# Scans of an attention and state-space block: diagonals of B through a DRAM buffer, three of eight token tiles

## The chip, the cores and the metric

The kernel runs on one core of a Trainium2 chip. The time is the device time of one execution in microseconds, from the chip's own clock; a lower one is better. All data are 32-bit floats.

## The reference

The input is an image of 256 x 256 tokens with 128 channels. Layer 0 adds row attention with four heads, layer 1 a two-dimensional state-space block; each works on a group-normed input. Nearly all the time goes to the scans of layer 1. The tokens are read in four orders k (by rows, by columns, and both backwards). For each order, each of 256 channels d and each of 16 states n, over the 65536 tokens t:

```python
def step(h, inp):
    d_t, x_t, B_t, C_t = inp
    dA = jnp.exp(d_t[..., None] * As)
    h = dA * h + (d_t * x_t)[..., None] * B_t[:, :, None, :]
    y = jnp.einsum('bkdn,bkn->bkd', h, C_t)
    return (h, y)
```

Here d_t = softplus(dts + dt_b) is a rate for each channel and token, x_t the token's 256 values, B_t and C_t are 16 numbers for each token. The four results are added, normed and projected back.

## The kernel before

The kernel has stages one after the other: statistics and norms, attention, a 3x3 convolution with the projections (`conv`), a transposition of a small array in DRAM (`swap`), the scans (`scans`), the output. The change is in `scans`; between the stages go arrays in DRAM, of which `bk` (B, one row of 16 floats for each token), `xk` (x), `dc0` and `dcT` (the low-rank rates and C) and `y` (the sum of the results) matter here.

**Tiling.** An order k is cut into 64 blocks of TB = 1024 tokens, which are NJ = 8 token tiles of 128. So there are 256 blocks. The first four and the last six blocks of an order are written out, the 54 between are three passes of a hardware loop over 18 blocks. Channels come in NH = 2 halves of 128, on the partitions of the scan. The work of a block is 32 units u = (state m, half h), each with these steps:

- `decay` (L837): ScalarE makes dA = exp(delta * A) for 1024 tokens, 4 units ahead.
- `scale` (L830): ScalarE makes what the turn needs, 3 states ahead. For the first DJ = 4 token tiles it writes into `dg` a diagonal 128 x 128 matrix with B of state m, that is the identity scaled per partition (L833). For the other four it writes into `but` the tile of d_t * x_t scaled by B (L835). In each half it does two of either.
- `turn` (L841): TensorE brings B * d * x to channels x tokens in PSUM, one unit ahead: a matmul of `dxt` with the diagonal for tiles below DJ (L846), a transposition of `but` for the others (L848). A matmul of floats stands as two instructions in the trace, a transposition as one.
- `recur` (L853): VectorE scans 1024 tokens (L858) and keeps the last state (L863); after the second half GpSimd multiplies both halves by C (L865), which `fetch` (L825) has loaded and spread over 128 partitions into one of four `cc` buffers, 3 to 4 states ahead.
- `collect` (L869): TensorE transposes the products and adds them up in PSUM over the states, three states behind (L617).

**The next block's preparation** is laid into the units of the present one (`begin`, L737): the rates by TensorE in units 6, 8, 18 and 20, a softplus from steps on ScalarE in units 6 to 12, on GpSimd in 11 to 14 and on VectorE in 18 and 20, its turn and the product with x in 22 and 24. These rates and turned rates use the same two PSUM buffers (`mms`) as the turns.

**Queues.** The order is written out by hand; every engine takes its instructions in that order. All loads and the store of y are issued by SP's queue, in the order in which the body names them: at unit 0 `load_tokens` for the next block (bt at L727, xk at L728, a megabyte), at unit 8 the store of the block before's y (L902, a megabyte), at 16 the load of y (L948, a megabyte), at 21 the rates (L724), and in each odd unit the cc for four states on (L826). A DMA whose target is not yet free keeps SP, and all that is behind it, waiting. The `dg`, `but` and `cc` rings have four buffers each, `da` and `hs` six.

Of the kernel before, what the change touches and what calls it, by code (L numbers as in the profile page):

```python
# [29 lines left out]
AF = mybir.ActivationFunctionType  # L30
# [5 lines left out]
P = 128  # L36
N = 256
# [4 lines left out]
NH = DI // P  # L42
DS = 16
# [576 lines left out]
def scans(tc, io, c):  # L620
# [11 lines left out]
    nc = tc.nc  # L632
    TB = 1024
    NJ = TB // P
# [5 lines left out]
    with tc.tile_pool(name="e_w", bufs=1) as wp, tc.tile_pool(name="e_1", bufs=1) as sb1, tc.tile_pool(  # L640
# [11 lines left out]
        def ring(name, n, shape, pool=wp):  # L652
            return [pool.tile(shape, F32, name=f"{name}{i}") for i in range(n)]

        DJ = NJ // 2
        xks = ring("xk", 1, [P, NJ, DI])

        dts = ring("dt", 1, [P, TB])
# [5 lines left out]
        ccs = ring("cc", 4, [P, TB])  # L664
        dgs = ring("dg", 4, [P, DJ, P])
        bus = ring("but", 4, [P, NJ - DJ, DI])
        das = ring("da", DA, [P, TB])
        hss = ring("hs", HS, [P, NH, TB])
# [16 lines left out]
        class Block:  # L685
# [39 lines left out]

            def load_tokens(self):
                nc.sync.dma_start(out=self.as_rows(self.bt), in_=self.rows(io["bk"][self.S.k]))  # L727
                nc.sync.dma_start(out=self.as_rows(self.xk), in_=self.rows(io["xk"]))  # L728

            def advance(self, now, after):  # L730
                if self.pieces is None:
                    self.pieces = begin(self)
                while self.pieces and self.pieces[0][:2] <= (now, after):
                    _, _, f, *args = self.pieces.pop(0)
                    f(*args)
# [89 lines left out]
        def fetch(B, m):  # L825
            nc.sync.dma_start(out=ccs[m % 4], in_=B.S.C[m : m + 1, B.where()].partition_broadcast(P))  # L826

        def scale(B, m, h):  # L830
            dg, bu = dgs[m % 4], bus[m % 4]
            for j in range(h * DJ // 2, (h + 1) * DJ // 2):
                nc.scalar.activation(dg[:, j, :], c.ident, AF.Copy, scale=B.bt[:, B.slot(j), m : m + 1])  # L833
                at = B.slot(DJ + j)
                nc.scalar.activation(bu[:, j, :], B.dxt[:, DJ + j, :], AF.Copy, scale=B.bt[:, at, m : m + 1])  # L835

# [4 lines left out]
        def turn(B, m, h):  # L841
            d1 = B.d1 = mm()
            dg, bu = dgs[m % 4], bus[m % 4]
            hc = slice(h * P, (h + 1) * P)
            for j in range(DJ):
                nc.tensor.matmul(d1[:, j * P : (j + 1) * P], B.dxt[:, j, hc], dg[:, j, :], start=True, stop=True)  # L846
# [6 lines left out]
        def recur(B, m, h):  # L853
            hs = hss[(B.n * DS + m) % HS]
            o, d0, d1 = hs[:, h, :], das[((B.n * DS + m) * NH + h) % DA], d1s.pop(0)
            if B.S.back:
                o, d0, d1 = o[:, ::-1], d0[:, ::-1], d1[:, ::-1]
            nc.vector.tensor_tensor_scan(o, d0, d1, state[:, m, h : h + 1], ALU.mult, ALU.add)  # L858
            if h == NH - 1:

                last = 0 if B.S.back else TB - 1
                last = hs[:, :, last : last + 1]
                nc.vector.tensor_reduce(state[:, m, :], last, AX.X, ALU.max)  # L863
                for x in range(NH):
                    nc.gpsimd.tensor_tensor(hs[:, x, :], hs[:, x, :], ccs[m % 4], ALU.mult)  # L865
# [16 lines left out]
        def collect_some(most):  # L882

            for x in list(waiting):
                if most == 0:
                    break
                B, _, _, j = x
                if B.slot(j) // PB in B.free:
                    waiting.remove(x)
                    collect(*x)  # L890
                    most -= 1

        def evict(B, after, part):

            n = NJ // PB // 2
            for g in range(part * n, (part + 1) * n):
                to = B.y[:, g * PB : (g + 1) * PB, :]
                nc.vector.tensor_tensor(to, to, pys[g], ALU.add)
                if after:
                    after.free.add(g)  # L900
            if part == 1:
                nc.sync.dma_start(out=B.rows(io["y"]), in_=B.as_rows(B.y))  # L902
# [5 lines left out]
        def body(blocks, before, after):  # L908

            own = len(blocks)  # L910
            at_hand = dict(enumerate(blocks + after))
            if before:
                at_hand[-1] = before
                before.free = before.started = set(range(NJ // PB))
                d1s[:] = [mms[count[0] % 2]]

            def at(u):
                x, s = divmod(u, U)
                return (at_hand[x], *divmod(s, NH)) if x in at_hand else None

            def do(f, u):
                if at(u):
                    f(*at(u))

            if before is None:
                blocks[0].load()
                blocks[0].load_tokens()
                blocks[0].advance(U, True)
                blocks[0].free = set(range(NJ // PB))
                blocks[1].load()  # L930
                for m in range(4):
                    fetch(blocks[0], m)
                for u in range(3 * NH):
                    do(scale, u)
                for u in range(4):
                    do(decay, u)
                do(turn, 0)
            for x, B in enumerate(blocks):
                nxt = at_hand.get(x + 1)
                for s in range(U):  # L940
                    u = x * U + s
                    m, h = divmod(s, NH)
                    if s == 0 and nxt:
                        nxt.load_tokens()
                    if s == 21 and x + 2 in at_hand:
                        at_hand[x + 2].load()
                    if s == 16:
                        nc.sync.dma_start(out=B.as_rows(B.y), in_=B.rows(io["y"]))  # L948
                    if nxt:
                        nxt.advance(s, False)  # L950
                    recur(B, m, h)
                    do(turn, u + 1)
                    if at(u - LAG * NH):
                        waiting.extend((*at(u - LAG * NH), j) for j in range(NJ))
                    collect_some(len(waiting) if s == LAG * NH - 1 else share.get(s, 10))
                    if x - 1 in at_hand and s in (6, 8):
                        evict(at_hand[x - 1], B, (s - 6) // 2)
                    if nxt:
                        nxt.advance(s, True)
                    do(decay, u + 4)  # L960
                    if u == 0:
                        nc.scalar.preload_act_table_set("natural_log_exp_and_others")
                    do(scale, u + 3 * NH)
                    if h == NH - 1 and at(u + 1 + 3 * NH):
                        fetch(*at(u + 1 + 3 * NH)[:2])
            if not after:
                waiting.extend((*at(u), j) for u in range(own * U - LAG * NH, own * U) for j in range(NJ))
                collect_some(len(waiting))
                for part in range(2):
                    evict(blocks[-1], None, part)  # L970
            assert not waiting
# [3 lines left out]
        passes = (n - 2) // LOOP  # L975
        first = (n - passes * LOOP) // 4 * 2
        order = [Scan(x, k) for x, k in enumerate((0, 2, 1, 3))]
        for x, S in enumerate(order):
            starts = [Block(S, b) for b in range(first)]
            ends = [Block(S, b) for b in range(first + passes * LOOP, n)]  # L980
            with tc.manual_schedule():
                nc.vector.memset(state, 0.0)
                body(starts, Block(order[x - 1], n - 1) if x else None, [Block(S, first + i) for i in range(2)])
            with tc.For_i(0, passes, 1, name=f"scan{S.k}") as it, tc.manual_schedule():  # L984
                body(
                    [Block(S, first + i, it) for i in range(LOOP)],
                    Block(S, first - 1, it),
                    [Block(S, first + LOOP + i, it) for i in range(2)],
                )
            with tc.manual_schedule():  # L990
                body(
                    ends,
                    Block(S, first + LOOP - 1, passes - 1),
                    [Block(order[x + 1], i) for i in range(2)] if x + 1 < len(order) else [],
                )


def output(tc, io, c):
# [73 lines left out]
    "dc1": (KD // 2 * RC, NT),  # L1072
    "dcT": (KD // 2 * RC, NT),
    "y": (NT, DI),
}


# [56 lines left out]
```

## Time and profile before

| | |
|---|---|
| median of 3 runs | 28440.62 us (28439.84 to 28441.89) |
| profiled execution | span 28447.5 us; no time beyond it is listed |
| busy: PE, DVE, ACT, POOL | 94%, 88%, 89%, 81% of the span |
| granted TensorE clock | 0.965 |
| DMA | 3630.07 MB, mean 128 GB/s; 1923996 packets |
| scans (L858), count and mean | 8192 of 2340 ns |
| diagonals on ACT (L833) | 16384 of 390 ns, 6393.1 us busy |
| scaled tiles on ACT (L835) | 16384 of 497 ns, 8150.2 us busy |

PE is TensorE, DVE VectorE, ACT ScalarE, POOL GpSimd and SP SyncE; PEld is the loading of TensorE's weights. A line such as L858 is a line of the kernel. In a row of a group the numbers behind the bar are the busy time in us and the mean ns of one instruction, then the time that the engine was idle just before them, and what ended most of it. In a timeline the columns are the start in us from the beginning of the span, the time that the row takes, the engine, the line, the operation, output and inputs, and how many instructions were merged; in square brackets the idle time before it and what ended it. ACT's instructions overlap a little, so that a unit's time is read from start to start. In a row of a DMA queue stand its packets, the MB and the share of sixteen engines' time. The scans take the span from about 4740 us to 27660 us.

### The profile page before, as it was taken

What the parts mean: (1) busy time and instruction counts of PE and PEld (TensorE: products, weight loads), DVE (VectorE), ACT (ScalarE), POOL (GpSimd) and SP (SyncE); (2) the same over time, 40 slices, a digit from 0 to 9 for tenths busy, and PEclk for the clock granted to TensorE, in tenths of its full rate; (3) what the DMA queues carried; (4) which work ended last, traced back from release to release, by engine and by line L of the source; (5) the groups of instructions that cost most, each with busy time, mean ns of one, the idle gap of its engine ahead of it and who ended that gap; (6) DMA issues with size and microseconds to landing.
All of it is one profiled execution on the core that took longest, in us unless ns stands there. A gap on an engine that the chain in (4) does not pass through costs nothing. (4 is left out here: it accounts for less than half of the span.)

```text
span 28447.5 us, 528099 instructions
## 1 busy us (share of the span) xinstructions
PE 26610.1 (94%) x196490; PEld 22529.2 (79%) x196490; DVE 24922.2 (88%) x24253; ACT 25332.4 (89%) x49673; POOL 22944.4 (81%) x10118
## 2 busy tenths in 40 slices
PE   8999996999999999999999999999999999999998
PEld 3555444888888888888888888888888888888884
DVE  4777665999999999999999999999999999999987
ACT  6875224999999999999999999999999999999987
POOL 2443002999999999999999999999999999999983
PEclk9999998999999999999999999999999999999999
DMA  5112345433433333333334333333333333333335
GB/s 206 55 50 71 111 116 115 132 132 129 133 130 133 132 131 132 132 131 132 128 132 133 131 133 132 131 132 129 132 132 130 133 132 129 132 130 132 133 132 172
DMA packets 1923996, 3630.07 MB, mean 128 GB/s; under 512 B 532297, under 2 KB 1240009, under 8 KB 1889490
## 3 DMA queue, kind: packets, MB, share of 16 engines
q1 hardware_dynamic: 1424722, 3339.77, 34.6%
q10 hardware_dynamic: 496640, 255.88, 3.2%
q8 instruction: 1568, 25.69, 0.4%
q14 instruction: 1066, 8.73, 0.1%
HBM read 3002.42 MB, written 592.84 MB: 126 GB/s over the span
## 5 line engine op out<-in xcount | busy, mean ns | idle before, releaser
L865 POOL TENSOR_TENSOR hs<-hs,cc 128x1024 f32<-128x1024 f32 x8192 | 19202.5, 2380 | 1346.1 <-DVE state L863 679.9
L858 DVE TENSOR_TENSOR_SCAN hs<-da,state,mm 128x1024 f32<-128x1024 f32 x8192 | 18976.6, 2340 | 1465.4 <-PE mm L848 1074.7
L846 PE MATMUL mm<-dg,dxt 128*128 128x128 f32 x65536 | 9305.0, 287 | 1065.1 <-DVE hs L858 886.1
L846 PEld LDWEIGHTS mm<-dg,dxt 128*128 128x128 f32 x65536 | 8328.4, 199 | 2257.9 <-DVE hs L858 1897.8
L839 ACT ACTIVATE da<-delta,A 128x1024 f32<-128x1024 f32 x8192 | 9328.4, 1139 | 112.2 <-PEq L984 76.0
L617 PE MATMUL y<-ident,hs 128*128 128x128 f32 x65536 | 8511.4, 275 | 1.4 <-POOL hs L865 1.4
L835 ACT ACTIVATE but<-dxt,bt 128x256 f32<-128x256 f32 x16384 | 8150.2, 497 | 11.4 <-DVE dxt L794 11.4
L617 PEld LDWEIGHTS y<-ident,hs 128*128 128x128 f32 x65536 | 7494.1, 143 | 1.9 <-POOL hs L865 1.9
L833 ACT ACTIVATE dg<-ident,bt 128x128 f32<-128x128 f32 x16384 | 6393.1, 390 | 0.2
L848 PE MATMUL mm<-ident,but 128*128 128x128 f32 x32768 | 5092.5, 280 | 0.0
L848 PEld LDWEIGHTS mm<-ident,but 128*128 128x128 f32 x32768 | 4011.4, 146 | 0.0
L750 PE MATMUL mm<-dt,dtw 9*128 9x512 f32 x4096 | 2033.0, 615 | 265.9 <-DMA bt<-mid_bk 184.5
L385 POOL TENSOR_TENSOR an<-ex,rs 128x1024 f32<-128x1024 f32 x512 | 970.2, 1895 | 1024.5 <-PE tp L394 566.3
L780 POOL TENSOR_TENSOR lw<-lw,e 128x1024 f32<-128x1024 f32 x512 | 1207.7, 2384 | 336.3 <-ACT lw L766 336.3
L750 PEld LDWEIGHTS mm<-dt,dtw 9*128 9x128 f32 x4096 | 680.7, 184 | 959.5 <-issue 733.3
L500 POOL MEMSET pad<- 128x10 f32 x32 | 3.7, 117 | 1650.0 <-PE ps L537 1639.9
L777 POOL TENSOR_TENSOR lw<-lw,w 128x1024 f32<-128x1024 f32 x512 | 1202.9, 2375 | 0.0
L537 PE MATMUL ps<-pad,w 128*128 128x512 f32 x2048 | 954.8, 610 | 161.0 <-ACT xi L525 161.0
L372 ACT ACTIVATE ex<-sc,nm 128x256 f32<-128x256 f32 x2048 | 1013.7, 499 | 0.4
L759 ACT ACTIVATE e<-mm 128x1024 f32<-128x1024 f32 x512 | 524.7, 1025 | 522.1 <-PE mm L750 521.9
L355 DVE CUSTOM_DVE_ANT_0 sc<-ps,bias 128x256 f32<-128x256 f32 x2048 | 746.2, 421 | 117.3 <-PE ps L340 117.3
L394 PEld LDWEIGHTS tp<-ident,an 128*128 128x128 f32 x4096 | 467.5, 141 | 470.7 <-POOL an L385 235.1
(137 smaller groups left out, 18522.4 us busy)
## 6 DMA issues: line engine op xcount, KB each, us to landing
cc<-mid_dc SPq DMA_DIRECT2D x2048, 512.0 KB
cc<-mid_dcT SPq DMA_DIRECT2D x2048, 512.0 KB
xk<-mid_xk SPq DMA_DIRECT2D x256, 1024.0 KB
yb<-mid_y SPq DMA_DIRECT2D x256, 1024.0 KB
mid_y<-yb SPq DMA_DIRECT2D x256, 1024.0 KB
xt<-mid_xT SPq DMA_DIRECT2D x64, 1024.0 KB
mid_xk<-xk ACTq DMA_DIRECT2D x32, 2048.0 KB
mid_y<-y ACTq DMA_DIRECT2D x32, 2048.0 KB
```

The source lines that it names most:

```text
L372: nc.scalar.activation(exs[u][:, x, :], scs[u][:, e, jt, :], AF.Exp, scale=-1.0, bias=nms[u][:, e, jt : jt + 1], accum_out=sms[u][:, x : x ...
L617: nc.tensor.matmul(out, in_, c.ident, is_transpose=True, start=start, stop=stop, skip_group_check=True)
L750: nc.tensor.matmul(pu[:, q : q + T], dtw[0 : DR + 1, k, h * P : (h + 1) * P], B.dt[0 : DR + 1, q : q + T], start=True, stop=True,)
L777: nc.gpsimd.tensor_tensor(B.lw[:, h, :], B.lw[:, h, :], B.w[:, h, :], ALU.add)
L780: nc.gpsimd.tensor_tensor(B.lw[:, h, :], B.lw[:, h, :], B.e[:, h, :], ALU.add)
L833: nc.scalar.activation(dg[:, j, :], c.ident, AF.Copy, scale=B.bt[:, B.slot(j), m : m + 1])
L835: nc.scalar.activation(bu[:, j, :], B.dxt[:, DJ + j, :], AF.Copy, scale=B.bt[:, at, m : m + 1])
L839: nc.scalar.activation(da, B.delta[:, h, :], AF.Exp, scale=A[:, B.S.k * NH + h, m : m + 1])
L846: nc.tensor.matmul(d1[:, j * P : (j + 1) * P], B.dxt[:, j, hc], dg[:, j, :], start=True, stop=True)
L848: nc.tensor.transpose(d1[:, j * P : (j + 1) * P], bu[:, j - DJ, hc], c.ident)
L858: nc.vector.tensor_tensor_scan(o, d0, d1, state[:, m, h : h + 1], ALU.mult, ALU.add)
L865: nc.gpsimd.tensor_tensor(hs[:, x, :], hs[:, x, :], ccs[m % 4], ALU.mult)
```

## The change

Three of the eight token tiles, instead of four, go through a diagonal (DJ = 3), and ScalarE makes none of them; it scales the five others, two in the first half of a state and three in the second. The diagonals come from a new DRAM array `dgd` with two parts, one for even and one for odd blocks; a part holds for each of the 16 states a matrix of 128 rows by 3 x 128 columns. Before the scans SP writes zeros into all of it. In `load_tokens`, between the loads of bt and xk, a new function `spread` issues three DMAs from DRAM to DRAM: each takes the 128 tokens by 16 states of one token tile from `bk` and writes every element into its place on the diagonal, a single float each, 2048 of them. The other places are zero from the start and stay so. `diagonal` then loads a state's whole 128 x 384 matrix into one of the four `dg` buffers (1536 bytes a partition, 192 KB). It is issued by SP in the even units after the scale, three states ahead, and for the first three states of all before the first unit.

```diff
@@ -652,7 +652,7 @@
         def ring(name, n, shape, pool=wp):
             return [pool.tile(shape, F32, name=f"{name}{i}") for i in range(n)]
 
-        DJ = NJ // 2
+        DJ = 3
         xks = ring("xk", 1, [P, NJ, DI])
 
         dts = ring("dt", 1, [P, TB])
@@ -725,7 +725,27 @@
 
             def load_tokens(self):
                 nc.sync.dma_start(out=self.as_rows(self.bt), in_=self.rows(io["bk"][self.S.k]))
+                self.spread()
                 nc.sync.dma_start(out=self.as_rows(self.xk), in_=self.rows(io["xk"]))
+
+            def diagonals(self):
+                return io["dgd"][self.b % 2]
+
+            def spread(self):
+                d = self.diagonals()
+                of = io["bk"][self.S.k]
+                G = N // P
+                with nc.allow_non_contiguous_dma(reason="one element of B per diagonal place"):
+                    for j in range(DJ):
+                        if self.S.across:
+                            x = of.rearrange("(g p w) c -> p g w c", p=P, w=N)
+                            x = x[:, j % G, self.where(N), :][:, j // G, :]
+                        else:
+                            x = of[self.where(), :].rearrange("(j p) c -> p j c", p=P)[:, j, :]
+                        to = bass.AP(
+                            d.tensor, d.offset + j * P, ((DJ * P + 1, P), (P * DJ * P, DS), (1, 1))
+                        )
+                        nc.sync.dma_start(out=to, in_=x.unsqueeze(2))
 
             def advance(self, now, after):
                 if self.pieces is None:
@@ -825,12 +845,15 @@
         def fetch(B, m):
             nc.sync.dma_start(out=ccs[m % 4], in_=B.S.C[m : m + 1, B.where()].partition_broadcast(P))
 
+        def diagonal(B, m):
+            nc.sync.dma_start(out=dgs[m % 4].rearrange("p j q -> p (j q)"), in_=B.diagonals()[m])
+
 
 
         def scale(B, m, h):
-            dg, bu = dgs[m % 4], bus[m % 4]
-            for j in range(h * DJ // 2, (h + 1) * DJ // 2):
-                nc.scalar.activation(dg[:, j, :], c.ident, AF.Copy, scale=B.bt[:, B.slot(j), m : m + 1])
+            bu = bus[m % 4]
+            nb = NJ - DJ
+            for j in range(h * nb // 2, (h + 1) * nb // 2):
                 at = B.slot(DJ + j)
                 nc.scalar.activation(bu[:, j, :], B.dxt[:, DJ + j, :], AF.Copy, scale=B.bt[:, at, m : m + 1])
 
@@ -930,6 +953,8 @@
                 blocks[1].load()
                 for m in range(4):
                     fetch(blocks[0], m)
+                for m in range(3):
+                    diagonal(blocks[0], m)
                 for u in range(3 * NH):
                     do(scale, u)
                 for u in range(4):
@@ -961,6 +986,8 @@
                     if u == 0:
                         nc.scalar.preload_act_table_set("natural_log_exp_and_others")
                     do(scale, u + 3 * NH)
+                    if h == 0 and at(u + 3 * NH):
+                        diagonal(*at(u + 3 * NH)[:2])
                     if h == NH - 1 and at(u + 1 + 3 * NH):
                         fetch(*at(u + 1 + 3 * NH)[:2])
             if not after:
@@ -975,6 +1002,12 @@
         passes = (n - 2) // LOOP
         first = (n - passes * LOOP) // 4 * 2
         order = [Scan(x, k) for x, k in enumerate((0, 2, 1, 3))]
+        nc.vector.memset(hss[0], 0.0)
+        for m in range(DS):
+            for x in range(2):
+                nc.sync.dma_start(
+                    out=io["dgd"][x, m], in_=hss[0].rearrange("p h t -> p (h t)")[:, 0 : DJ * P]
+                )
         for x, S in enumerate(order):
             starts = [Block(S, b) for b in range(first)]
             ends = [Block(S, b) for b in range(first + passes * LOOP, n)]
@@ -1072,6 +1105,7 @@
     "dc1": (KD // 2 * RC, NT),
     "dcT": (KD // 2 * RC, NT),
     "y": (NT, DI),
+    "dgd": (2, DS, P, 3 * P),
 }
```

## The prediction

> **What bounds the kernel now.** I read the page's busy times first, then its costliest groups, then the timelines of the engines over one block of the scans, and last the DMA windows.
>
> ```profile
> PE 26610.1 (94%) x196490; PEld 22529.2 (79%) x196490; DVE 24922.2 (88%) x24253; ACT 25332.4 (89%) x49673; POOL 22944.4 (81%) x10118
> ...
> L865 POOL TENSOR_TENSOR hs<-hs,cc 128x1024 f32<-128x1024 f32 x8192 | 19202.5, 2380 | 1346.1 <-DVE state L863 679.9
> L858 DVE TENSOR_TENSOR_SCAN hs<-da,state,mm 128x1024 f32<-128x1024 f32 x8192 | 18976.6, 2340 | 1465.4 <-PE mm L848 1074.7
> ```
>
> Four engines are almost level, so one block must be added up. There are 256 blocks (4 scans of 64), each of 16 states m by 2 halves h, 32 units. The loads of bt at L727 run from 4738.7 to 27493.6 us, one a block: (27493.6 - 4738.7) / 255 = 89.2 us a block.
>
> ACT, in its timeline, pays a unit of 2.43 us (next fence: 14255.26 to 14257.69), of which a dg takes 0.29 and a but 0.40. 32 x 2.43 = 77.8, four 128x2048 steps at 1.80 between starts are 7.2, two Abs at 0.92 are 1.8, and it waits 2.0 for the rates (L759, 521.9 us over 256). Sum 88.8: ACT is full. DVE has 18976.6 + 636.6 + 624.2 + 613.8 + 644.2 us (L858, L863, L783, L794, L898) / 256 = 84.0, and six places where a rate or a turned rate takes a PSUM buffer between two turns, about 0.6 each (the 0.61 below): 87.6. POOL has (19202.5 + 1207.7 + 1202.9) / 256 = 84.4. So a faster ACT can win little: DVE's chain stands 1.6 us behind it, POOL 4.8.
>
> ```profile
> 14255.26 1.13 ACT L839 ACTIVATE da<-delta,A 128x1024 f32<-128x1024 f32 x1
> 14256.30 0.39 ACT L833 ACTIVATE dg<-ident,bt 128x128 f32<-128x128 f32 x1
> 14256.59 0.49 ACT L835 ACTIVATE but<-dxt,bt 128x256 f32<-128x256 f32 x1
> 14256.99 0.39 ACT L833 ACTIVATE dg<-ident,bt 128x128 f32<-128x128 f32 x1
> ...
> 14257.69 1.13 ACT L839 ACTIVATE da<-delta,A 128x1024 f32<-128x1024 f32 x1
> ```
>
> What the change leans on is SP's queue, which issues in order. In the block whose first scan starts at 14255.39:
>
> ```profile
> 14261.27 0.33 SPq L826 DMA_DIRECT2D cc<-mid_dc  x1
> 14261.94 0.38 SPq L727 DMA_DIRECT2D bt<-mid_bk  x1
> 14262.71 0.38 SPq L728 DMA_DIRECT2D xk<-mid_xk  x1
> ...
> 14311.18 0.33 SPq L826 DMA_DIRECT2D cc<-mid_dc  x1
> 14311.84 0.38 SPq L948 DMA_DIRECT2D yb<-mid_y  x1
> ```
> ```profile
> 14269.57 2.35 DVE L858 TENSOR_TENSOR_SCAN hs<-da,state,mm 128x1024 f32<-128x1024 f32 x1
> 14271.83 1.26 DVE L898 TENSOR_TENSOR yb<-yb,y 128x512 f32<-128x512 f32 x2
> 14273.70 2.35 DVE L858 TENSOR_TENSOR_SCAN hs<-da,state,mm 128x1024 f32<-128x1024 f32 x1 [0.61 <-PE mm L848]
> ...
> 14316.48 2.35 DVE L858 TENSOR_TENSOR_SCAN hs<-da,state,mm 128x1024 f32<-128x1024 f32 x1
> ```
>
> The cc at 14261.27 is that of m=3, and 14269.57 is the scan of m=3, h=0; the cc at 14311.18 and the scan at 14316.48 belong to m=11. Each cc waits on SP for POOL to finish m-4 (SP's waits: L826 for POOL, 19503.2 us in 4092 waits), so its lead is POOL's lag: 8.3 us here, only 5.3 at m=11, where POOL's four softplus operations have put it behind. That is harmless now: POOL reads cc after the scan. A diagonal is read by the turn before it.
>
> **What is removed.** On ACT four dg a state go and a fifth but comes: 4 x 0.69 = 2.76 becomes 5 x 0.40 = 2.0, or 12 us a block. Only what ACT holds up comes back: 1.6 us to DVE's chain (not less than 0, not more than the 4.8 to POOL). On PE one diagonal matmul of four becomes a transpose. With the clock full (last fence) four diagonals take 0.89 and four transposes 0.44, so a turn goes from 1.49 to about 1.38. This counts only in DVE's six gaps, 0.7 at most, partly the same time. Together I take 2.0.
>
> **What is added at m=3.** At the start of a block SP issues bt, now three spreads, and xk; behind them comes the diagonal of m=3. Each spread writes 2048 single floats, 385 floats apart; 3 x 2048 / 16 = 384 places for each DMA engine. No row of before copies 4 bytes between two DRAM places. Below stands the nearest, the 64-byte stores of bk with the queue to themselves from 4134 to 4139 us:
>
> ```profile
> q10 hardware_dynamic: 6809, 0.43, 81.8%
> ```
>
> 6809 / 16 engines / 5 us is 11.75 ns a place, which makes the three 4.5 us. The bound above is the 1024-byte row: xk's 1024 packets need about 49 ns each on an engine, 18.8 us; the bound below is that they are hidden. I take 11.75, the nearest in size. xk's packets end at 14269.6 now (224 packets under 2 KB in the microsecond from 14268, 39 in the next), so with the spreads ahead at 14274.1. Packets of one queue follow one another on each engine: the cc issued at 14265.94 runs out only with xk. The diagonal adds eight rows of 1536 B an engine, between the 1024-byte row's 49 ns and the 4096-byte row's 189, about 0.6 us, and 0.3 for its completion (an estimate): 14275.0. Then the turn, 1.4 us, or 2.7 if PE has cooled: after 10.15 us of idleness at a loop's edge its granted clock is 0.50 and the same work takes twice the time:
>
> ```profile
> 14074.59 2.07 PE L846 MATMUL mm<-dg,dxt 128*128 128x128 f32 x8 [10.15 <-PEq L984]
> 14076.45 1.06 PE L848 MATMUL mm<-ident,but 128*128 128x128 f32 x4
> ...
> 14081.43 1.06 PE L846 MATMUL mm<-dg,dxt 128*128 128x128 f32 x8
> 14082.32 0.60 PE L848 MATMUL mm<-ident,but 128*128 128x128 f32 x4
> 14082.76 1.04 PE L617 MATMUL y<-ident,hs 128*128 128x128 f32 x8
> ```
>
> The scan then starts at 14276.4 to 14277.7 in place of 14269.57: 6.8 to 8.1 us late. I take 7.5. PE's collects wait behind that turn, DVE behind PE, POOL behind DVE; nothing else feeds DVE, so it is all on the path.
>
> **What is added at m=11.** yb's megabyte is issued between the cc and the diagonal of m=11. Its packets end at 14317.6 (124 under 2 KB in the microsecond from 14317, 15 in the next); with 0.9 for the diagonal and a turn of 1.4 to 2.7 the scan starts at 14319.9 to 14321.2, not 14316.48: 3.4 to 4.7, I take 4.0. The store of y before the diagonal of m=7 costs nothing: in this block it is issued at 14282.53, 9.7 us ahead of that scan at 14292.24, against about 6 for its megabyte, 0.9 and a turn. Elsewhere a diagonal follows its cc by 0.7 us with some 8 us in hand and lands in about 5 (3.3 from a cc's issue to its last row, and 0.7 + 0.9); DMA engines are 39% busy, and 16 x 0.6 plus 4.5 us a block adds 16 points.
>
> **Once.** 32 stores of zeros, 6.3 MB, go ahead of the first load on SP, where PE is idle anyway and everything waits: at 6 us a megabyte 38 us (49 at the page's mean 128 GB/s, 0 if hidden).
>
> **Sum.** A block gains 2.0 and loses 7.5 + 4.0: +9.5 us, by 256 is 2432, and 38: +2470. The profiled execution has a span of 28447.5 us and no time beyond it is listed; the runs' median is 28440.62, 6.9 less. 28440.6 + 2470 = 30910.
>
> A rule speaks against the change. The Trainium skill, "DMA: Bandwidth & Descriptors", section "Rules for kernel authors", says that a strided last dimension lowers to one descriptor per element and should be rearranged; the trace's 64-byte stores agree that small pieces are paid by number, and no run here shows 4 bytes. The same page's fit of 2.0 us plus bytes over 436 GB/s (section "Anatomy of one DMA", made for another issue path) would give three spreads of 8 KB in a row 6.0 us, an estimate, and a total of about 31300 in place of 30910.
>
> **Rivals.** *The spreads are hidden.* If the single floats go out beside other packets, only xk and yb stand before the diagonals: at m=3 the scan comes 2.3 to 3.6 us late, 3.0, so 3.0 + 4.0 - 2.0 = +5.0 a block: 29760. For it: the DMA engines are 61% free. Against it: the queue shows one DMA after another.
>
> *The spreads are dear.* At 49 ns a place 14.3 us more a block: 34580. For it: a 4-byte write to DRAM is nowhere in the trace. Against it: 64-byte pieces cost 11.75.
>
> *Faster.* If a diagonal does not queue behind the megabytes, only the relief of ACT is left: 28440.6 - 256 x 2.0 + 38 = 27970. It decides from where the diagonal of m=3 lands within 6.2 us of bt's issue (7.6 less a turn) and that of m=11 within 3.2 of yb's. Against it: xk alone ends 7.7 after bt's issue, yb 5.8 after its own.
>
> **How the numbers follow.** Likeliest 0.58 (its own range 30000 to 32000: the bounds of both delays, the relief at 0 or 3.5); hidden spreads 0.14; dear 0.18; faster 0.08; all cancelling to within 0.2%, about what a measurement here can tell from nothing, 0.02. Hidden spreads reach down to about 29100, and half of the dear case lies under 34600: that range leaves out some 2 in 10. Faster 0.08, same 0.02, slower 0.90.
>
> **What would show it.** In the profile after: DVE's scan waits for PE, and PE's first matmul of a turn for a DMA into dg, about twice a block, near 7 and 4 us; the granted clock has more halves; ACT has some 12 us a block idle; about 1.57 million packets of 4 bytes more, near 12 ns each; POOL's share falls with the longer span. Wrong would be no wait of PE for dg (the relief alone), or waits of 20 us at m=3 (dear floats), or waits at every m.

## The result, and the profile after

The changed kernel takes 33757.21 us (median of 4 runs, 33705.18 to 33802.12) against 28441.25 us before (median of 4 runs in the same comparison). The ratio is 1.187, with a 95% interval of 1.185 to 1.189. The prediction said slower, 30910 us; the loss is 5316 us where 2470 were forecast.

The page of the changed kernel, its busy times, its clock and the groups that answer to those shown of before:

```profile
PE 27119.3 (80%) x188298; PEld 22660.9 (67%) x188298; DVE 24970.1 (74%) x24254; ACT 22599.4 (67%) x37385; POOL 22928.5 (68%) x10118
...
PEclk9999978888888888888888888888888888888889
...
q1 hardware_dynamic: 3604306, 4157.97, 41.0%
...
L881 DVE TENSOR_TENSOR_SCAN hs<-da,state,mm 128x1024 f32<-128x1024 f32 x8192 | 18953.7, 2339 | 6569.3 <-PE mm L871 6122.0
...
L869 PE MATMUL mm<-dg,dxt 128*128 128x128 f32 x49152 | 7962.7, 302 | 5889.6 <-DMA dg<-mid_dgd 5084.8
```

VectorE does the same scans in the same time, but it now waits 6569 us before them, not 1465; it waits for TensorE, and TensorE waits 5085 us for the DMA that brings `dg`. No engine is level with the span any more.

Where in a block does that wait lie? The starts of the scans give the time in us from one unit's scan to the next one's, as a mean over 254 of the 256 blocks (the first and the last of all are left out):

| unit | before | after | difference |
|---|---|---|---|
| 5 to 6 (scan of m=3) | 2.46 | 16.31 | +13.85 |
| 6 to 7 | 4.18 | 5.73 | +1.55 |
| 21 to 22 (scan of m=11) | 2.47 | 9.21 | +6.74 |
| the 29 others together | 80.3 | 79.1 | -1.2 |
| block | 89.4 | 110.4 | +21.0 |

21.0 us by 256 blocks is 5376, within about 1% of the measured loss of 5316. Both places are those of the prediction. The SP queue around m=3 of one block, in its timeline (start, time, line, DMA, count):

```profile
11401.50 0.33 SPq L846 DMA_DIRECT2D cc<-mid_dc  x1
11401.92 0.39 SPq L727 DMA_DIRECT2D bt<-mid_bk  x1
11402.36 5.54 SPq L748 DMA_DIRECT2D mid_dgd<-mid_bk  x3
11408.00 3.58 SPq L729 DMA_DIRECT2D xk<-mid_xk  x1
11411.67 2.17 SPq L849 DMA_DIRECT2D dg<-mid_dgd  x1
```

The same stretch on TensorE and VectorE:

```profile
11407.28 1.04 PE L617 MATMUL y<-ident,hs 128*128 128x128 f32 x8
11421.38 1.62 PE L869 MATMUL mm<-dg,dxt 128*128 128x128 f32 x6 [13.06 <-DMA dg<-mid_dgd]
11422.78 1.27 PE L871 MATMUL mm<-ident,but 128*128 128x128 f32 x5
```
```profile
11424.19 2.35 DVE L881 TENSOR_TENSOR_SCAN hs<-da,state,mm 128x1024 f32<-128x1024 f32 x1 [13.37 <-PE mm L871]
```

The diagonal of m=3 is issued at 11411.67, and TensorE has it at 11421.38, 19.5 us after bt was issued. Even issuing has become slow: the spreads, xk and this diagonal hold SP for 5.54, 3.58 and 2.17 us, where xk took 0.38 before. The three diagonal matmuls (six instructions) then take 1.62 us; at m=10 of the same block, in the first TensorE row below, they take 0.94. Around m=11 of the same block:

```profile
11466.35 0.33 SPq L846 DMA_DIRECT2D cc<-mid_dc  x1
11466.73 0.43 SPq L973 DMA_DIRECT2D yb<-mid_y  x1
11467.25 0.53 SPq L849 DMA_DIRECT2D dg<-mid_dgd  x1
```
```profile
11466.99 0.94 PE L869 MATMUL mm<-dg,dxt 128*128 128x128 f32 x6
...
11474.71 1.62 PE L869 MATMUL mm<-dg,dxt 128*128 128x128 f32 x6 [5.91 <-DMA dg<-mid_dgd]
```

### The profile page after: what moved, and what is told of

It reads as the page before. It is cut to its first block, busy times and chain, and to the rows that moved or that the text cites. A ratio compares the mean times of both kernels' runs of the same rounds, so it can differ in the third digit from the quotient of the medians.

```text
span 33799.6 us, 511644 instructions
## 1 busy us (share of the span) xinstructions
PE 27119.3 (80%) x188298; PEld 22660.9 (67%) x188298; DVE 24970.1 (74%) x24254; ACT 22599.4 (67%) x37385; POOL 22928.5 (68%) x10118
## 5 line engine op out<-in xcount | busy, mean ns | idle before, releaser
L869 PE MATMUL mm<-dg,dxt 128*128 128x128 f32 x49152 | 7962.7, 302 | 5889.6 <-DMA dg<-mid_dgd 5084.8
L869 PEld LDWEIGHTS mm<-dg,dxt 128*128 128x128 f32 x49152 | 6696.2, 207 | 7397.7 <-issue 5359.9
L858 ACT ACTIVATE but<-dxt,bt 128x256 f32<-128x256 f32 x20480 | 8970.3, 496 | 93.4 <-PE mm L871 81.0
L617 PE MATMUL y<-ident,hs 128*128 128x128 f32 x65536 | 8892.0, 283 | 1.9 <-POOL hs L888 1.9
L617 PEld LDWEIGHTS y<-ident,hs 128*128 128x128 f32 x65536 | 7892.2, 148 | 2.4 <-POOL hs L888 2.4
L871 PE MATMUL mm<-ident,but 128*128 128x128 f32 x40960 | 6312.1, 289 | 0.6 <-ACT but L858 0.4
L871 PEld LDWEIGHTS mm<-ident,but 128*128 128x128 f32 x40960 | 5205.8, 151 | 1.5 <-ACT but L858 1.5
L770 PE MATMUL mm<-dt,dtw 9*128 9x512 f32 x4096 | 2171.7, 651 | 283.6 <-DMA bt<-mid_bk 202.6
L547 DVE SCALAR_TENSOR_TENSOR acc<-xi,cw,acc 128x512 f32<-128x512 f32 x1024 | 754.3, 749 | 28.2 <-issue 1.6
```

What stands on the lines that cost most here:

```text
L617: nc.tensor.matmul(out, in_, c.ident, is_transpose=True, start=start, stop=stop, skip_group_check=True)
L770: nc.tensor.matmul(pu[:, q : q + T], dtw[0 : DR + 1, k, h * P : (h + 1) * P], B.dt[0 : DR + 1, q : q + T], start=True, stop=True,)
L871: nc.tensor.transpose(d1[:, j * P : (j + 1) * P], bu[:, j - DJ, hc], c.ident)
```

## The experiments

The theory under test is called Q: nothing costs but the order of SP's queue. A diagonal lands when all that was issued ahead of it has gone through, and what was too small in the prediction is the price of the spreads' single floats. The kernel before was run beside every one of them (28438 to 28444 us). Experiments one to four, down to the wait at m=11, ran on one chip, the others on another; the changed kernel was not run again beside them, so a difference from its 33757 us may be one between chips too. All but the last two versions below have a single run.

### Are the single floats the price?

Experiment one leaves the spreads out:

```diff
                 nc.sync.dma_start(out=self.as_rows(self.bt), in_=self.rows(io["bk"][self.S.k]))
-                self.spread()
                 nc.sync.dma_start(out=self.as_rows(self.xk), in_=self.rows(io["xk"]))
```

> The changed kernel without the three spreads a block; the diagonals are loaded as before but stay zero, so three token tiles add nothing to the result. Theory Q (the number of 4-byte places standing in the queue ahead of xk and of the diagonal of m=3): the late scan of m=3, 16.3 us after the one before it in place of 2.5, comes down to some 5.5 (xk ends 7.1 after bt's issue, 1.6 for the diagonal and its completion, 2.7 for a cold turn, 6.2 already gone), so 10.8 us a block less: 33757 - 2760 = 31000. Rival R (the spreads cost the 4.5 us that was predicted, the rest comes from the diagonals' own loads behind xk and from the cold TensorE): 4.5 us a block less, 32600.

Measured 30341.94 us, 3415 less than the changed kernel and below what Q expected. The step to m=3 is 3.8 us on the mean, not 5.5: in three of four blocks TensorE is still at full clock after the short wait, and from the turn's first matmul to the scan 1.6 us pass, where the changed kernel always needs 2.8. The spreads thus cost 12.5 us at m=3 (16.31 - 3.79), not 4.5, and rival R falls.

The second writes the same bytes in longer pieces:

```diff
-                        to = bass.AP(
-                            d.tensor, d.offset + j * P, ((DJ * P + 1, P), (P * DJ * P, DS), (1, 1))
-                        )
-                        nc.sync.dma_start(out=to, in_=x.unsqueeze(2))
+                        to = bass.AP(d.tensor, d.offset + j * P, ((DJ * P, P), (1, DS)))
+                        nc.sync.dma_start(out=to, in_=x)
```

> The changed kernel, each spread writing the same 8 KB to the same DRAM buffer as 128 rows of 64 bytes in place of 2048 single floats (the matrices are then not diagonals and the result is not that of the reference). Theory Q (paid by the number of places): 24 places an engine and block, 0.3 us in place of 9.0; near the kernel without spreads, 31000 to 31200. Rival D (paid by copying from DRAM to DRAM, or by three more DMAs with their issue and latency): stays over 33000.

Measured 30934.17 us. Three DMAs from DRAM to DRAM of the same 24 KB cost 592 us over the whole run against none (2.3 us a block); cut into single floats they cost 3415. It is the cutting into single floats that is paid, and rival D falls. As the bytes are the same, the number of the pieces and their size change together here.

### Do they cost anything when nobody waits behind them?

The third adds the buffer, its zeros and `spread` to the kernel before, where ScalarE makes the diagonals:

```diff
                 nc.sync.dma_start(out=self.as_rows(self.bt), in_=self.rows(io["bk"][self.S.k]))
+                self.spread()
                 nc.sync.dma_start(out=self.as_rows(self.xk), in_=self.rows(io["xk"]))
```

> The kernel before (ScalarE makes four diagonals) with the zeros and the three spreads a block added, which nobody reads. Theory Q (a spread costs only through the diagonal that waits behind it): the next cc has 11 us in hand and is read after the scan, so about 28440 + 40 for the zeros, at most 28700. Rival C (the single floats take the DMA engines or DRAM from everything else, or block SP): cc and xk come late too, 29500 or more.

Measured 28463.08 us, 25 us over the kernel before. Its group of scans has the idle time of the kernel before:

```profile
L878 DVE TENSOR_TENSOR_SCAN hs<-da,state,mm 128x1024 f32<-128x1024 f32 x8192 | 18978.3, 2340 | 1459.5 <-PE mm L868 1056.2 <-ACT dg L853 177.0 <-PEq L1010 79.7
```

So 1.57 million single floats, in the same place of the same queue, cost next to nothing while what stands behind them is not needed soon: the 25 us hold the zeros, and the seven runs of the kernel before in one comparison already lie 18 us apart. The floats do delay xk, whose last row comes 16.6 us after bt's issue in place of 7.2 (medians of the row-wise scans), but it is first used in unit 22. Rival C falls: the floats take no time from the engines' other work.

### The wait at m=11

```diff
-                    if s == 16:
-                        nc.sync.dma_start(out=B.as_rows(B.y), in_=B.rows(io["y"]))
 ...
                     if h == 0 and at(u + 3 * NH):
                         diagonal(*at(u + 3 * NH)[:2])
+                    if s == 16:
+                        nc.sync.dma_start(out=B.as_rows(B.y), in_=B.rows(io["y"]))
```

> The changed kernel with one move: the load of y in unit 16 is issued behind the diagonal of m=11 and not ahead of it. Theory Q: the wait at m=11 goes (9.2 us from scan to scan back to 2.5), 6.7 us a block: 33757 - 1715 = 32040; the wait at m=3 stays at 16.3. Rival L (at m=11 the diagonal is late because its cc waits for GpSimd, which is behind by its softplus steps, not because of y): at least 4 us of the wait stay, or move to m=12: 33000 or more.

Measured 32022.78 us, 1734 less. The sum is what Q expected, but the parts are not, and that it fits is luck. The step to m=11 is 4.5 us on the mean, so that 4.7 of the 6.7 us are gone and 2.0 are left; and the step to m=3, which the move does not touch and which was to stay at 16.3, is 14.1. The 4.7 us are some 1200 us of the 1734, and the 2.2 us at m=3 make up the rest.

The second part is the spreads, which cost less here: xk's last row comes 16.5 us after bt's issue, as in experiment three (16.6) on the same chip, against 18.7 in the changed kernel, whose chip is not on record, and 18.7 on the other chip in the kernel with the diagonals four states ahead (medians of the row-wise scans). That fits a difference between chips; it was not tested apart. The 12.5 us and the 3415 us of experiment one, set against the changed kernel's own runs, would then be some 2.2 us a block smaller on its own chip, and still far above rival R's 4.5.

So most of the wait at m=11 is the load of y. Rival L's price, 4 us or more, falls; the 2.0 us that stay, with only the cc ahead of the diagonal, can be its share.

### What does a single float cost, and why?

The trace shows what the spreads do to the queue. The three fences give the GB/s of the DMA engines in 40 slices of 0.5 us, beginning where bt is issued. First without spreads (experiment one):

```profile
GB/s 0 213 344 295 225 124 191 282 305 369 387 387 399 393 415 380 293 111 0 74 213 328 289 318 184 70 0 0 41 287 344 211 238 260 61 0 0 0 0 0
```

The cc and bt fill the first slices, then xk runs at up to 415 GB/s and is through after some 9 us in this block. In the changed kernel:

```profile
DMA  0799999700022457735431534587989999999999
GB/s 0 115 328 328 248 140 34 5 1 0 1 2 2 3 4 4 3 2 3 3 2 1 13 17 61 37 92 84 221 209 305 311 314 312 385 393 402 413 411 413
```

The upper row is the busy share of the DMA engines in tenths. Counted from 0, slices 7 to 21 have hardly anything but floats, at most 5 GB/s. After a quick burst the engines are all but idle for a microsecond and a half (slices 8 to 10), though SP is still issuing spreads, and then busy for one to seven tenths of the time. A float's own packet takes 8.8 ns, 3.4 us for the 384 of an engine; for most of the stretch the queue is not busy with them, it stands. And xk then begins slowly too. Over the row-wise blocks xk's last row comes 18.7 us after bt's issue (median), 7.2 without spreads: 11.5 us for 384 floats on each engine, 30 ns apiece. By the 16.5 and 16.6 us of experiments four and three it is 24.

To see whether it is a price for each float, one spread in place of three:

```diff
-                    for j in range(DJ):
+                    for j in range(1):
                         if self.S.across:
```

> The changed kernel with one of the three spreads a block (tokens of the first tile alone get their diagonal; the two other tiles add nothing). Theory A (every single float costs the same 23 ns, so the three spreads' 12.5 us at m=3 are shared evenly): the scan of m=3 comes 4.2 us later than without spreads, 3.8 + 4.2 = 8.0 us after the one before it: 30342 + 1070 = 31400. Theory E (the first 2048 floats go at the 11.75 ns of the 64-byte stores and only what follows at once is slow): some 2 us: 30850.

Measured 31767.42 us: above both. The step to m=3 is 8.7 us, 5.0 more than without spreads, which would be 39 ns a float. But only 4.0 of them are the queue's: xk's last row comes 11.1 us after bt's issue in place of 7.2, 31 ns a float, the same price as for three spreads. The other microsecond is TensorE, which is at half clock in this turn in every block and without spreads was so in one of four; and the step behind it is 0.9 us longer too. So theory A is right that every float costs the same, and wrong in the 23 ns and in leaving out the clock. The queue, from the issue of bt:

```profile
DMA  0297999704358998849999999999999989500010
GB/s 0 90 377 262 288 144 30 5 0 8 20 109 133 117 88 111 59 100 236 313 383 333 346 412 423 422 399 422 387 368 362 356 331 355 211 12 0 0 33 0
```

The 2048 floats do go out at once, 1267 in the microsecond from 3 to 4 us after bt (mean of 100 blocks), 12.6 ns apiece on an engine, near the 11.75 ns of the prediction. But then the queue all but stands for about a microsecond (slices 8 and 9), and xk, which moves at about 400 GB/s without spreads, begins at 100. Theory E is right about the burst and wrong about the price: a float that has left the queue is not paid yet.

Is it where they are written?

```diff
-((DJ * P + 1, P), (P * DJ * P, DS), (1, 1))
+((DJ * P, P), (8, DS), (1, 1))
```

> The changed kernel with the same 6144 single floats a block, but the sixteen floats of a token 32 bytes apart in one row of one matrix, not one in each of sixteen matrices 196608 bytes apart (so the matrices are not the diagonals that the result needs). Theory A (a single float costs 23 ns on a DMA engine wherever it goes): 33757 within 300. Theory B (far-apart places cost; 11.75 ns, as 64-byte stores, when they are near): 4.5 us a block less from the places and 2 to 3 from xk behind them: 31900 to 32600.

Measured 37123.17 us. Neither theory expected that: near places are much dearer, 13.1 us a block more than far ones, and TensorE's wait for `dg` is 8358.0 us:

```profile
L869 PE MATMUL mm<-dg,dxt 128*128 128x128 f32 x49152 | 7980.6, 303 | 9175.6 <-DMA dg<-mid_dgd 8358.0 <-DVE hs L881 611.5 <-PEq L1017 79.4
```

Is it the step of 196608 bytes, a multiple of 65536?

```diff
-    "dgd": (2, DS, P, 3 * P),
+    "dgd": (2, DS, P * 3 * P + PAD),
 ...
-((DJ * P + 1, P), (P * DJ * P, DS), (1, 1))
+((DJ * P + 1, P), (P * DJ * P + PAD, DS), (1, 1))
```

> The changed kernel with every matrix in DRAM followed by 4224 unused bytes, so that the sixteen places of a token are 200832 bytes apart and no longer a multiple of 65536. Theory A (a single float has its price) and theory B (far apart is dear): 33757 within 300. Theory C (the multiple of 65536 sends them all to the same part of the memory): as near places, 31900 to 32600.

Measured 33875.86 us; theory C falls. And is it the reading or the writing?

```diff
                 nc.sync.dma_start(out=self.as_rows(self.bt), in_=self.rows(io["bk"][self.S.k]))
-                self.spread()
                 nc.sync.dma_start(out=self.as_rows(self.xk), in_=self.rows(io["xk"]))
+                self.spread()
 ...
-                            x = of[self.where(), :].rearrange("(j p) c -> p j c", p=P)[:, j, :]
+                        x = self.bt[:, self.slot(j), :]
```

> The changed kernel with the spreads behind xk and their source the tile bt in SBUF, which SP first waits for. If reading single floats out of DRAM is what costs (theory D), the places take 4.5 us behind an xk that ends 7.2 after bt's issue: the diagonal lands at about 13.5, the scan of m=3 comes at about 16 in place of 22.6: 32100. If writing them costs (theories A to C): 9 us behind xk, 18 and 20.5 to 21: 33200 to 33400.

Measured 32973.78 us, between the two and nearer to the second: the step to m=3 is still 13.2 us. So reading single floats out of DRAM is not the larger part. Whether the 3.1 us that are gone come from the new source or from the new order behind xk was not separated, and a source in SBUF is still read in single floats. That their place changes the price so much says that the destination has to do with it; what the memory does with them was not seen in these runs and stays open. It is not the destination alone: with the near places the step to m=3 is 26.3 us in the row-wise and 33.0 in the column-wise scans (medians), and only the order in which the floats are read differs between them.

### Can the queue be put in an order in which nothing waits?

First one move alone:

```diff
-                    if h == 0 and at(u + 3 * NH):
-                        diagonal(*at(u + 3 * NH)[:2])
+                    if h == 0 and at(u + 4 * NH):
+                        diagonal(*at(u + 4 * NH)[:2])
 ...
```

> The changed kernel with one move: each diagonal is issued four states ahead in place of three, so before the cc that waits for GpSimd; the spreads and the three megabytes stay where they are. Theory Q: the diagonal of m=12 now follows the load of y, with 7.2 + 4.7 us in hand, so the wait at m=11 goes (6.7 us a block); behind the spreads and xk stands the diagonal of m=4, which has 4.7 us more, so of 13.8 us at m=3 some 9 stay, at m=4: 33757 - 256 x 11.4 = 30840, between 30300 and 31300. Rival (a late cc, not the diagonal's place, holds TensorE): 33000 or more.

Measured 30574.72 us. The wait at m=11 is gone (2.46 us from unit 21 to 22), and the one at m=3 has become 8.0 us at m=4, 10.5 us from unit 7 to 8. Four `dg` buffers allow that distance, because the turn of m is done when the diagonal of m+4 is issued. Then everything together (the lines that are taken out of their old places, the spreads' among them, are left out here):

```diff
                     if h == 0 and at(u + 4 * NH):
                         diagonal(*at(u + 4 * NH)[:2])
+                    if s == 0 and nxt:
+                        nxt.load_tokens()
+                    if s in (2, 4, 6) and nxt:
+                        nxt.spread([s // 2 - 1])
+                    if s == 16:
+                        nc.sync.dma_start(out=B.as_rows(B.y), in_=B.rows(io["y"]))
 ...
```

> Each diagonal is issued one state earlier (four ahead, so before the cc that waits for GpSimd); bt and xk of unit 0 and the load of y of unit 16 go behind the diagonal of their unit; the three spreads go one each behind the diagonals of units 2, 4 and 6. Theory Q (only the order in the queue costs): a spread takes some 3 us of a queue that is busy 2.9 of 4.7 us a state, with 13 us in hand: no wait for a diagonal is left, VectorE's own chain of 86.8 us a block bounds: 28440 - 256 x 1.6 + 25 = 28050, between 27900 and 28300. Rival C (the single floats delay all that is in flight): the wait spreads over m = 4 to 7, over 29000.

Measured 28278.36 us (median of 4), a ratio of 0.994 to the kernel before with an interval of 0.9925 to 0.9959: 0.6% faster than before, with every float and every diagonal load still there. No wait for `dg` is left among what ended TensorE's idle time:

```profile
L880 DVE TENSOR_TENSOR_SCAN hs<-da,state,mm 128x1024 f32<-128x1024 f32 x8192 | 18950.7, 2339 | 1221.1 <-PE mm L870 777.2 <-ACT but L857 208.6 <-PEq L1019 81.2
L861 ACT ACTIVATE da<-delta,A 128x1024 f32<-128x1024 f32 x8192 | 9368.4, 1144 | 1540.2 <-DVE hs L880 1184.7 <-PEq L1019 100.8 <-DMA cc<-mid_dcT 24.0
...
L868 PE MATMUL mm<-dg,dxt 128*128 128x128 f32 x49152 | 7748.6, 297 | 1348.8 <-DVE hs L880 1108.6 <-PEq L1019 81.0 <-DMA cc<-mid_dcT 19.5
```

ScalarE now waits for VectorE (1184.7 us), which it hardly did before. It stays 228 us above the expected 28050. VectorE's chain is 87.9 us a block in the row-wise scans (the sum of the median steps), not 86.8; the steps that are longer than expected are those out of units 6, 18 and 20, where the rates and turns come, and the half-clock stretches have grown from 1977 us in all to 2306. That a TensorE with less to do cools more often is the likely reason; it was not tested apart. The last run gives the diagonals two tiles in place of three (DJ = 2, two spreads):

```diff
-        DJ = 3
+        DJ = 2
 ...
-                    if s in (2, 4, 6) and nxt:
+                    if s in (2, 4) and nxt:
```

> The rearranged kernel (diagonals four ahead, spreads apart) with two token tiles through diagonals in place of three; ScalarE scales six. ScalarE has some 10 us a block to spare and pays 6.4 of them. If VectorE's chain bounds through the turns in its six gaps, each is 0.11 us shorter: 28278 - 170 = 28110. If TensorE, with less to do, falls to half clock more often (it was at half clock for 2306 us in the rearranged kernel, 1977 in the one before), that eats the gain: 28250 to 28350.

Measured 28122.42 us (median of 4), a ratio of 0.989, interval 0.987 to 0.990. The first guess held in its sum: with ScalarE no longer the bound, shorter turns pay, and ScalarE has room for a sixth scaled tile (85% busy, 80% with three diagonals). Of the six steps the four out of units 18, 20, 22 and 24 are 0.10 to 0.15 us shorter on the mean, near the 0.11 expected; the one out of unit 6 is 0.38 shorter and the one out of unit 8 0.24 longer. TensorE was at half clock for longer again, 2541 us, and that did not eat the gain. This is the best version of the study.

## Why the prediction was right and wrong

**What bounds the kernel.** Right. ScalarE was full, and to free it is worth little: with no wait left the gain was 163 us. The prediction's relief of 2.0 us a block was somewhat large: the units of the changed kernel that have no wait are 1.2 us a block shorter, and the rearranged kernel as a whole gains 0.6.

**m=3, the step that failed.** Mechanism, queue and place were as predicted, the size was not: 13.85 us and not 7.5. The term is "which makes the three 4.5 us", the 11.75 ns a place taken from the 64-byte stores. Measured, the three spreads put off the end of xk by 11.5 us (18.7 against 7.2), 30 ns a place. A rate near 12 ns is true of the first 2048 floats, and it is the wrong thing to count: it tells how fast the queue hands floats on, not when the queue moves again. The upper bound of 18.8 us held the value. Two smaller terms nearly cancel: from xk's last row to the scan 3.9 us passed, for which the prediction had 2.9 (landing 0.9 and a turn of 1.4 to 2.7; TensorE was always cold; no run shows the 0.3 us that were added for the completion by themselves), and the unhindered scan would have come 8.7 us after bt's issue over the blocks, not 7.6 as in the one block that was read. 11.5 - 4.5 - 0.5 for the end of xk, which is 7.2 and not 7.7, + 1.0 - 1.1 = 6.4: 7.5 + 6.4 = 13.9.

**m=11.** Right in kind, 6.74 us and not 4.0. Here the one block that was read was a lucky one: its y came in 5.8 us with 4.6 in hand, where the changed kernel's medians are 6.45 and 3.9 (the second from the units' usual step), and the last step took 3.9 and not 2.9. Experiment four took 4.7 us of the wait away; all of it went only when the diagonal was issued a state earlier.

**What was not in the sum.** 1.55 us from unit 6 to 7, right behind the long wait. The changed kernel's TensorE is at half clock for 7317 us, before for 1977. The prediction counted the cold turn alone, not the work behind it: the matmuls of the rates take 651 ns on the mean in place of 615, which is 0.6 us over all the units of a block. Where the rest of the 1.55 us lies was not traced.

**The rest.** The store of y ahead of m=7 costs nothing (2.46 us from unit 13 to 14, before 2.48). The zeros cost 17 us until the first scan (4797.95 in place of 4780.74), not 38; with the unread spreads of experiment three the whole run is 25 longer, zeros and spreads together.

**The rivals.** "Hidden" is out: even without any float the time is 30342, over its 29760. "Dear" had the right term and came to 34580 with 49 ns a float; 30 were measured. "Faster" needs diagonals that do not queue behind the megabytes. They do queue; but issued in another order they need not, and then something near it happened (28278 against 27970).

## What to carry to other kernels

Here a DMA that a compute engine waited for landed after what was issued ahead of it in its queue; before a load is added, write down what stands in front of it at each place of the loop and how long each takes, as a median over blocks and not from one. Scattered single floats should be priced by when the next DMA behind them moves, not by the rate at which their packets go out; put them where nothing behind them is needed soon: there they cost at most 25 of 28440 us here. When an engine that was full is relieved, look again at the split that was tuned for it: here two tiles in place of three then paid about as much again (156 us) as the relief with three had (163).

## What was not expected of the hardware

Single floats written 32 bytes apart into one row are dearer than the same number written 196608 bytes apart (37123 against 33757 us in all, 13.1 us a block), while a padded step changes nothing much (33876). A burst of 2048 floats over 16 DMA engines goes out at some 12.6 ns apiece and is followed by a stretch in which the queue stands with work in it; the load behind it begins at a quarter of its usual rate. And SP itself is held up behind the spreads: the issue of a one-megabyte load took 3.58 us where it took 0.38 without them. Last, the price of a float was not the same everywhere: the same three spreads put xk off by 9.3 us on one chip and by 11.5 on the other, over whole runs.
